# A bidirectional scan layer on one core: one conv tap of two residues moved from TensorE to VectorE, order of residues 1, 2, 3, 0, gates made one pair ahead

## The chip, the cores and the metric

One core of a Trainium2 chip runs the kernel alone. The metric is the device time of one launch in microseconds (us). It was run three times; the table below gives the median. The profile comes from one further execution, whose own span is given beside it.

## The reference, cut to what matters

The input x is (4, 128, 96, 96) in float32. Each image is normalized in 32 groups of channels, and then read as four sequences of length L = 9216: along rows (H), along columns (V), and both of these backwards. On each sequence runs the same layer:

```python
t = grouped1x1(x, in_proj_w, in_proj_b, 4)        # 128 -> 512 channels
u, gate = t[:, :256], t[:, 256:]
u = silu(u)
u = depthwise_conv(u, dw_w, kernel=5, padding=2)   # 256 channels
s = ssm_in_w @ u                                   # 32 channels
a = DMIN + (DMAX - DMIN) * sigmoid(ssm_delta_w @ u + ssm_delta_b)
bb, cc = tanh(ssm_b_w @ u + ssm_b_b), tanh(ssm_c_w @ u + ssm_c_b)
h[l] = a[l] * h[l-1] + bb[l] * s[l]                # the recurrence, as a scan
u = u + ssm_out_w @ (cc * h + ssm_d * s)
y = out_proj_w @ grouped1x1(u * sigmoid(gate), mix_w, mix_b, 4)
```

The four results, put back in image order, are joined to 512 channels, mixed to 128 by fuse_w, and added to x. All of it is float32.

## The kernel before, in words

**Tiling.** A sequence is cut into 6 steps of 16 lines (1536 positions), and within a step into 4 residues p = 0..3: the positions 4n + p, N = 384 of them. A unit is one direction, one step, one residue. A pair t holds the two units s = 0 and 1 that run at the same time: a forward sequence from its start and the matching backward sequence from the other end. Image by image, first V and then H make 8 phases of 24 pairs, 192 pairs in all. So pair t has step t // 4 and, as its residue, k = t % 4.

**Mirrored steps.** The backward sequence meets the positions of the forward one in the second half of a phase. So in_proj and silu are computed only in a phase's steps 0 to 2 ("fresh"); steps 3 to 5 read the same silus backwards, from SBUF for step 3 and through DRAM copies (kept_sil) for steps 4 and 5. In the same way the gates are computed for the first 12 pairs of a phase, ten of these twelve tiles are kept in DRAM, and the last 12 pairs take them in mirrored order.

**One pair, pair() at L797.** The parts of a pair are spread over time: front (in_proj and silu, L403 to L484) runs four pairs ahead; conv, taps and proj belong to pair t itself; ssm_out, the gating and the output product belong to pair t - 6 (LAG) and t - 7.

- The 256 conv channels come as two halves j. Half j = 1 is convolved on ScalarE and VectorE: the first tap (L648, ScalarE, into PSUM banks 0 and 1) and four taps (L650, VectorE, the last one into u). Half j = 0 is convolved on TensorE: since the sequence lies as residues, channels of 32 by 4 residues make 128 rows, and one product with a banded 128x32 matrix (conv, L610) takes all taps that lie in the same shift k of n; the taps that lie in the neighbouring shift are a second product over 64 rows (conv_less, L619). For residues 1 and 2 that second product holds two taps' rows; for residues 0 and 3 only one of the five taps lies there. ScalarE then copies the result to u (L629 or L631).
- proj (L662) multiplies u for s, delta, b and c: 16 products into banks 4 and 5, then two tanh and a copy on ScalarE (L687, L688, L693), decay and the product b * s on GpSimd (L695, L696), and scale_s on ScalarE (L705).
- recurrence (L786): in the first two pairs of a step VectorE scans the two halves of the step before (L722); GpSimd forms cc * h + d * s of pair t - 5 (outputs, L726).
- under (L509) copies u of pair t - 6 to the PSUM banks of ssm_out (0 and 1 for s = 0, 2 and 3 for s = 1); out_of (L501) adds ssm_out's product; gate (L487) makes the gates' products, ScalarE their tanh (L521), each for the pair that uses them at once; gating (L582, L597) is one VectorE instruction per unit, (gate + 1) * PSUM, written over u.
- accumulate (L742) makes the fused product of mix, out_proj and fuse for the unit gated a pair before, ScalarE copies it out of PSUM (ys, L755 or L757), and GpSimd adds it to acc, the image in SBUF (L774). Complete regions of acc leave for DRAM (L737) and are loaded with the next image (L827).

**What sets the order.** All engines' orders are written out by hand (manual_schedule); each engine executes its instructions in program order and waits on semaphores. All transfers but one are issued by SyncE, on one queue: x_in for fronts (L269) and gates (L284), the kept silus (L450, L457) and gates (L530, L538), chunks of the next image for its statistics (L383), and acc. The banks are shared: taps and ssm_out of s = 0 use 0 and 1; proj uses 4 and 5; conv uses 4 and 5 or 7 and 6, the accumulates the other two; the gates 4 to 7.

**Kinds of pair** by t % 24: 0 to 5 and 20 to 23 have a front, 8 to 17 have gates, 6 and 7 both, 18 and 19 neither.

## Time and profile before

| what | value |
|---|---|
| median of 3 runs | 1809.4 us (1809.08 to 1810.35) |
| profiled execution: span from first to last instruction | 1812.7 us |
| TensorE (PE) busy, share of the span | 99% |
| ScalarE (ACT) | 86% |
| VectorE (DVE) | 80% |
| GpSimd (POOL) | 79% |
| transfers on the SyncE queue | 317.48 MB, 54.4% of the 16 DMA engines' span |

How to read the views that follow. A group row gives line, engine, operation, the tiles written and read with their shapes, the count, then busy time in us, the mean of one in ns, and the idle time of that engine just before them with what ended it. A matmul's record is its own duration; up to four, eight or sixteen run side by side in column and row tiles, so a group's busy time is less than count times mean. A timeline row gives start and length in us, engine, line and operation, and merges neighbours of one kind (x16). A float32 product appears as two instructions, so conv's 8 products of a pair are 16. Line numbers are those of the kernel before.

### The profile page before, as it was taken

The page shows a single profiled execution, that of the slowest core. Times are in us where ns is not written, and L with a number is a line of the kernel's source. Part 1 is how long each engine was busy: PE and PEld are TensorE (multiplying, and loading weights), DVE is VectorE, ACT ScalarE, POOL GpSimd, SP SyncE. Part 2 cuts the span into 40 slices and gives each one's busy share as a digit, 9 for nine tenths or more (in the row PEclk, how much of TensorE's full clock was granted, in tenths as well). Part 3 has the DMA queues.
Part 4 walks back from the last instruction along what each step waited for, and adds up shares of the span by engine and source line. Part 5 has one row for each costly group of instructions (what it writes and reads, how often), then busy time and mean ns, then how long its engine had stood idle before and what let it go on. Part 6 is the DMA issues. An engine that isn't in the chain of part 4 may idle for free.

```text
span 1812.7 us, 56970 instructions
## 1 busy us (share of the span) xinstructions
PE 1788.9 (99%) x24090; PEld 645.3 (36%) x24090; DVE 1446.5 (80%) x1462; ACT 1567.0 (86%) x2750; POOL 1432.0 (79%) x1477
## 2 busy tenths in 40 slices
PE   6999999999999999999999999999999999999998
PEld 3333333333333333333333333333333333333333
DVE  5888878887888887877788888787877878777886
ACT  4988888998888888898988888889888888889975
POOL 3587887778778888788877888778778788887876
PEclk9999999999999999999999999999999999999999
DMA  7655463444975466344696447443477734645434
GB/s 229 183 184 196 149 185 117 163 145 142 305 246 188 159 177 204 102 145 141 204 306 225 159 161 211 138 146 119 160 232 223 249 118 150 192 122 176 148 112 175
DMA packets 148047, 321.17 MB, mean 177 GB/s; under 512 B 14160, under 2 KB 115920, under 8 KB 147792
## 3 DMA queue, kind: packets, MB, share of 16 engines
q1 hardware_dynamic: 147648, 317.48, 54.4%
q8 instruction: 190, 3.11, 0.7%
q14 instruction: 65, 0.53, 0.1%
q10 hardware_dynamic: 144, 0.04, 0.0%
HBM read 185.21 MB, written 132.25 MB: 175 GB/s over the span
## 4 chain that ended last, share of the span: by engine, by line
PE 95%; DMA 2%; DVE 2%; ACT 1%; issue 0%; SPq 0%; DVEq 0%
PE psum L134 82%; PE psum L504 8%; PE psum L491 5%; DVE psum L650 1%; DMA x_in<-in_xs 1%; DMA xs<-in_xr 1%; DMA acc<-in_xr 0%; DVE u L597 0%; DVE u L650 0%; ACT psum L512 0%; PE psum L1035 0%; ACT u L631 0%; SPq L296 0%; ACT ys L757 0%; DVE bn L387 0%
## 5 line engine op out<-in xcount | busy, mean ns | idle before, releaser
L650 DVE SCALAR_TENSOR_TENSOR psum<-sil,small,psum 128x768 f32<-128x768 f32 x576 | 589.0, 1023 | 28.4 <-ACT psum L648 3.4
L597 DVE SCALAR_TENSOR_TENSOR u<-gate,psum 128x768 f32<-128x768 f32 x376 | 350.0, 953 | 273.4 <-ACT u L629 119.0
L134 PE MATMUL psum<-u,w_fin 128*32 128x384 f32 (+1 forms) x6192 | 551.1, 485 | 1.6 <-ACT ys L755 1.2
L134 PE MATMUL psum<-u,main 128*32 128x384 f32 x6144 | 534.7, 489 | 1.5 <-DVE u L650 1.4
L774 POOL TENSOR_TENSOR acc<-ys,acc 128x384 f32<-128x384 f32 x375 | 411.6, 1119 | 24.0 <-ACT ys L757 7.9
L728 POOL TENSOR_TENSOR t<-t,t 64x384 f32<-64x384 f32 (+1 forms) x192 | 237.7, 1238 | 156.9 <-DVE t L722 73.2
L134 PEld LDWEIGHTS psum<-u,w_fin 128*32 128x32 f32 x6192 | 189.3, 109 | 319.6 <-issue 215.3
L134 PEld LDWEIGHTS psum<-u,main 128*32 128x32 f32 x6144 | 181.9, 109 | 324.7 <-issue 197.2
L512 ACT COPY psum<-u 128x768 f32<-128x768 f32 x352 | 277.3, 801 | 17.5 <-DVE u L650 11.5
L134 PE MATMUL psum<-sil,band 128*32 128x384 f32 x3072 | 285.1, 488 | 0.0
L695 POOL TENSOR_SCALAR t<-tm 64x384 f32<-64x384 f32 x191 | 176.9, 926 | 117.3 <-ACT tm L687 97.9
L729 POOL TENSOR_TENSOR t<-t,t 64x384 f32<-64x384 f32 (+1 forms) x192 | 249.1, 1297 | 15.0
L504 PE MATMUL psum<-t,main 32*128 32x384 f32 x1536 | 238.6, 513 | 1.3 <-ACT psum L512 0.6
L648 ACT ACTIVATE psum<-sil,small 128x768 f32<-128x768 f32 x191 | 173.7, 909 | 56.2 <-DVE u L597 48.0
L521 ACT ACTIVATE gate<-psum,bnorm 128x384 f32<-128x384 f32 x384 | 192.2, 584 | 26.5 <-PE psum L491 25.5
L696 POOL TENSOR_TENSOR t<-t,tm 64x384 f32<-64x384 f32 x192 | 195.3, 1017 | 15.3
L650 DVE SCALAR_TENSOR_TENSOR u<-sil,small,psum 128x768 f32<-128x768 f32 x192 | 194.9, 1015 | 7.8
L470 ACT ACTIVATE sil<-psum,bnorm 128x385 f32<-128x385 f32 x384 | 192.6, 585 | 7.1 <-PE psum L134 4.8
L134 PE MATMUL psum<-sil,less 64*32 64x384 f32 x3072 | 168.1, 495 | 0.0
L491 PE MATMUL psum<-x_in,wn 32*128 32x384 f32 x768 | 157.3, 527 | 0.0
L134 PEld LDWEIGHTS psum<-sil,band 128*32 128x32 f32 x3072 | 90.6, 109 | 169.2 <-issue 94.4
L731 POOL COPY t<-t 64x384 f32<-64x384 f32 x187 | 136.8, 731 | 11.9
(103 smaller groups left out, 1480.3 us busy)
## 6 DMA issues: line engine op xcount, KB each, us to landing
sil<-sil SPq DMA_DIRECT2D x128, 770.0 KB, 6.7
kept<-gate SPq DMA_DIRECT2D x80, 768.0 KB, 3.7
gate<-kept SPq DMA_DIRECT2D x76, 768.0 KB, 4.9
x_in<-in_xs SPq DMA_DIRECT2D x192, 96.2 KB, 2.5
out<-acc SPq DMA_DIRECT2D x48, 384.0 KB, 8.2
acc<-in_xr SPq DMA_DIRECT2D x39, 384.0 KB, 6.8
xs<-in_xr SPq DMA_DIRECT2D x72, 192.0 KB, 5.7
x_in<-in_xs SPq DMA_DIRECT2D x46, 192.5 KB, 3.5
```

Source lines behind the costliest of these rows:

```text
L134: nc.tensor.matmul(o[r, : rhs.shape[-1]], lhsT, rhs, start=start, stop=stop, skip_group_check=True)
L470: nc.scalar.activation(sils[step][:, s, j, g, :], bank(bk)[:, : N + 1], AF.Silu, bias=bn[:, 1:2] if j else bn[:, 4 + g : 5 + g],)
L491: nc.tensor.matmul(bank(to)[:, :N], stats[un["b"]][0][r, s, :], x_in[s][r, q, off : off + N], start=True, stop=True)
L504: nc.tensor.matmul(bank(ssm(bi, s) + j)[:, :N], w_so[r, bass.ts(j, P)], z[r, :], start=bi not in seeded, stop=True, skip_group_check=True)
L512: nc.scalar.copy(psum[:, ssm(bi, s) : ssm(bi, s) + 2, :N], us[bi][:, s])
L521: nc.scalar.activation(gv[:, s, j, :], bank(to[2 * s + j])[:, :N], AF.Tanh, bias=bn[:, 2 + j : 3 + j], scale=0.5,)
L597: nc.vector.scalar_tensor_tensor(v, g, 1.0, pz, ALU.add, ALU.mult)
L650: nc.vector.scalar_tensor_tensor(us[i][:, :, 1, :] if k == K - 1 else part, src, w_tap[:, k : k + 1], part, ALU.mult, ALU.add,)
L696: nc.gpsimd.tensor_mul(ta[0:64, p, :], tb[0:64, :], tm[0:64, :])
L728: engine.tensor_mul(ta[0:64, p, r], tb[64:P, r], ta[64:P, p, r])
L729: engine.tensor_add(tb[0:64, r], ta[0:64, p, r], tb[0:64, r])
L774: adder.tensor_add(part, y, part)
```

## The change

- For t from 8 on, pair() gives way to a new pair_on().
- Residues 0 and 3 ("lone" pairs, alone(p)): conv closes its accumulation, conv_less and its copy are left out, and add_lone, one VectorE instruction, multiplies the one missing tap's silus by its weight, adds conv's PSUM banks and writes u. The silus of the neighbouring residue lie on other partitions than needed; so keep_lone stores the 32 partitions of each edge residue to DRAM (edge_sil, four DMAs per fresh step), and load_lone fetches them in a layout of 128 channels by 4 slots into one buffer, once per step.
- The order of residues is 1, 2, 3, 0 (TURN), so the lone pairs are the third and the fourth of a step. The scans stay in the first two.
- The gates of pair n + 1 are made beside ssm_out of pair n, and all 12 tiles of a half phase are kept in DRAM. Those of a phase's first three pairs are made at t % 24 = 17, 18, 19 of the phase before, in a tile that the start-up weights used (shared), and fetched later. So the pairs with a front (t % 24 = 20 to 23 and 0 to 7) make no gates, and the other 12 make them all. Two of the four tanh become one 768-wide instruction.
- In every pair from 8 on, u is copied under ssm_out on ScalarE (under), never added by VectorE.
- tm has one buffer instead of two, xs three instead of four; the statistics of the next image are spread as one chunk per pair, and finished in more and smaller pieces, two per pair.

The core of the diff:

```diff
+TURN = (1, 2, 3, 0)
...
+    def alone(p):
+        return p in (0, R - 1)
...
+    def keep_lone(step):
+        for e, r in enumerate((slice(96, P), slice(0, 32))):
+            for s in range(2):
+                nc.sync.dma_start(
+                    edge_of(step)[2 * e + s].rearrange("g c n -> c g n"), sils[step][r, s, 0, :, :]
+                )
+
+    def load_lone(step):
+        lone[step] = wk.tile([P, 4, N + 1], F32, tag="lone", bufs=1, name=f"lone_{step}")
+        nc.sync.dma_start(lone[step], edge_of(step).rearrange("a g c n -> (g c) a n"))
+
+    def add_lone(i, banks):
...
+        nc.vector.scalar_tensor_tensor(
+            us[i][:, :, 0, :],
+            columns(step, slots, k),
+            w_edge[:, 1 - k : 2 - k],
+            psum[:, banks[0] : banks[0] + 2, :N],
+            ALU.mult,
+            ALU.add,
+        )
...
+    def pair_on(t):
...
+        if mirror(n + 1) is None and (n + 1) % NP > 2:
+            gated = n + 1
+            to = tile_of(gated)
+        elif t % NP in (17, 18, 19) and t + LAG + 1 < end:
+            gated = t + LAG + 1
+            to = shared()[:, : 4 * N].rearrange("p (s j n) -> p s j n", s=2, j=2)
+        banks, w = (PROJ, FRONT[:2]) if fronted else ((6, 7), PROJ)
...
+        front(t + R, FRONT)
...
+        if k == 0 and fresh(un["step"]):
+            keep_lone(un["step"])
+        if k == (1 if fresh(un["step"]) else 0):
+            load_lone(un["step"])
+        if not fronted:
+            under(bi, 1)
...
+        taps(i, range(1, K))
+        conv(i, banks, single)
+        if single:
+            add_lone(i, banks)
+        recurrence(t)
+        stats_chunks(t)
...
+        if fronted:
+            under(bi, 1)
+            under(bi, 0)
...
+        adds = [accumulate(waiting.pop(0), w[0], *adder)]
+        if not late:
+            adds[0]()
+        if not fronted:
+            if not single:
+                conv_less(i, banks)
+            under(bi, 0)
+        adds.append(accumulate(waiting.pop(0), w[1], *adder))
...
+        if fronted:
+            if not single:
+                conv_less(i, banks)
+            scale_s(i - 2)
...
+        gate_of(1, 1, 4)
+        out_of(bi, 0, 0)
+        out_of(bi, 0, 1)
+        out_of(bi, 1, 1)
+        gate_of(1, 0, 7)
+        gate_of(0, 0, 6)
+        out_of(bi, 1, 0)
+        gate_of(0, 1, 5)
+        for s in range(2):
+            gating(bi, s)
+            if s == 0 and gated is not None:
+                tanh_one(gated, to, 1, 1, 4)
+                tanh_one(gated, to, 0, 1, 5)
+        first_tap(i + 2)
+        if gated is not None:
+            tanh_both(gated, to, 0, 6)
+            nc.sync.dma_start(kept[gated // NP % 2][gated % NP], to)
...
+        proj(i, PROJ, not fronted)
+        if not fronted:
+            scale_s(i - 2)
```

More of the change, by code (lines that the diff above doesn't have):

```diff
@@ L98, in conv_preact_kernel @@
         for st in range(NS):
-            for p in range(R):
+            for k, p in enumerate(TURN):
                 for s in range(2):
@@ L365, in conv_preact_kernel @@
     kept = [
-        [dp.tile([P, 2, 2, N], F32, tag=f"kept{e}_{m}", name=f"kept{e}_{m}") for m in range(NP // 2 - 2)]
+        [dp.tile([P, 2, 2, N], F32, tag=f"kept{e}_{m}", name=f"kept{e}_{m}") for m in range(NP // 2)]
         for e in range(2)
@@ L375, in chunks_of @@
         b, k = un["b"] + 1, t % R
-        if un["order"] == "V" and b < B and k > 1:
-            return [(b, un["st"] * R + 2 * (k - 2) + e) for e in range(2)]
+        if un["order"] == "V" and b < B:
+            m = t % NP
+            first = m - 2 + (m > 10) + (m > 18)
+            return [(b, first + e) for e in range(1 + (m in (10, 18)))] if m > 1 else []
         return []
@@ L472, in silu, with silu_both @@
             bank(bk)[:, : N + 1],
+            AF.Silu,
+            bias=bn[:, 1:2] if j else bn[:, 4 + g : 5 + g],
+        )
+    def silu_both(step, g, j, b0):
+        bn = stats[units[step * UB]["b"]][1]
+        nc.scalar.activation(
+            sils[step][:, :, j, g, :],
+            psum[:, b0 : b0 + 2, : N + 1],
             AF.Silu,
@@ L492, in gate, with gate_tile @@
                          start=True, stop=True)
+    def gate_tile(n, s, j, to, c):
+        un = units[2 * n + s]
+        q, off = gate_at(un)
+        r = slice(64 * (1 - s) + 32 * j, 64 * (1 - s) + 32 * j + 32)
+        mm(bank(to), c, stats[un["b"]][0][r, s, bass.ts(c, 32)], x_in[s][r, q, off : off + N],
+           True, True)
     turning = (6, 0, 2)
@@ L608, in blocks, with conv @@
         return [sils[step][:, s if fresh(step) else 1 - s, 0] for s in range(2)]
-    def conv(i, banks):
+    def conv(i, banks, alone=False):
         step, p = units[i]["step"], units[i]["p"]
@@ L631, in conv_less, with less_both @@
             nc.scalar.copy(us[i][:, :, 0, :], psum[:, b0 : b0 + 2, :N])
+    def less_both(i, banks):
+        step, p = units[i]["step"], units[i]["p"]
+        sil, k = blocks(step), less_of(p)
+        for g in range(4):
+            for s in range(2):
+                r = less_rows(s, p)
+                mm(bank(banks[s]), g, less[r, p, g, :], columns(step, sil[s][r, g, :], k), False, True)
     def new_u(i):
@@ L660, in conv_preact_kernel, with proj @@
     qb, qc, qa, qs = (slice(MH * i, MH * (i + 1)) for i in range(4))
-    def proj(i, banks, apart=False):
+    def proj(i, banks, apart=False, between=None):
         step, p = units[i]["step"], units[i]["p"]
@@ L1116, in conv_preact_kernel @@
         start()
-        for t in range(NU // 2):
+        for t in range(LAG + 2):
             pair(t)
+        for t in range(LAG + 2, NU // 2):
+            pair_on(t)
         tail()
```

200 lines of the change are left out of this document (165 added, 35 removed).

## The prediction, made blind

> **What bounds the kernel now.** I read the profile from the top: the busy shares, then the chain that ended last.
>
> ```profile
> PE 1788.9 (99%) x24090; PEld 645.3 (36%) x24090; DVE 1446.5 (80%) x1462; ACT 1567.0 (86%) x2750; POOL 1432.0 (79%) x1477
> PE 95%; DMA 2%; DVE 2%; ACT 1%; issue 0%; SPq 0%; DVEq 0%
> ```
>
> TensorE is busy for 99% of the span of 1812.7 us and is 95% of the chain. So the time is the length of its instruction stream, and the reader should next see how one pair of units is made up. The timeline of a pair with gates but without a front (columns: start, us, engine, line):
>
> ```profile
> 353.39 0.59 PE L491 MATMUL psum<-x_in,wn 32*128 32x384 f32 x2
> 354.97 2.79 PE L134 MATMUL psum<-u,main 128*32 128x384 f32 x32
> 357.57 1.47 PE L134 MATMUL psum<-sil,band 128*32 128x384 f32 x16
> 358.86 1.47 PE L134 MATMUL psum<-u,w_fin 128*32 128x384 f32 x16
> 359.45 0.79 ACT L512 COPY psum<-u 128x768 f32<-128x768 f32 x1
> 360.26 0.88 PE L134 MATMUL psum<-sil,less 64*32 64x384 f32 x16
> 360.40 0.58 ACT L755 ACTIVATE ys<-psum,b_fin 128x384 f32<-128x384 f32 x1 [0.17 <-PE psum L134]
> 361.07 1.50 PE L134 MATMUL psum<-u,w_fin 128*32 128x384 f32 x16
> 361.25 0.80 ACT L631 COPY u<-psum 128x768 f32<-128x768 f32 x1 [0.26 <-PE psum L134]
> 361.94 0.81 ACT L512 COPY psum<-u 128x768 f32<-128x768 f32 x1
> 362.50 0.59 PE L491 MATMUL psum<-x_in,wn 32*128 32x384 f32 x2
> ```
>
> From start to start on TensorE: gates and ssm_out together ("the wave") 1.58, proj 2.60, band 1.29, first accumulate 1.40, less 0.81, second accumulate 1.43. The pair takes 362.50 - 353.39 = 9.11 us. Write O for the start of the wave. Then the copy of conv's result (L631) starts at O + 7.86, as soon as less is done, and the copy of u under s = 0 (L512) ends at 362.75, which is 0.25 after the next wave began. The old order bears that, because its two ssm_out products of s = 0 come last but one in the wave. A pair with a front and without gates, from proj to proj:
>
> ```profile
> 417.67 2.77 PE L134 MATMUL psum<-u,main 128*32 128x384 f32 x32
> 420.36 0.95 PE L134 MATMUL psum<-x_in,wn 32*32 32x385 f32 x32
> 421.24 1.50 PE L134 MATMUL psum<-sil,band 128*32 128x384 f32 x16
> 422.55 2.76 PE L134 MATMUL psum<-u,w_fin 128*32 128x384 f32 x32
> 423.64 1.54 ACT L512 COPY psum<-u 128x768 f32<-128x768 f32 x2
> 425.25 0.88 PE L134 MATMUL psum<-sil,less 64*32 64x384 f32 x16
> 426.05 0.93 PE L504 MATMUL psum<-t,main 32*128 32x384 f32 x8
> 426.91 2.79 PE L134 MATMUL psum<-u,main 128*32 128x384 f32 x32
> 427.10 1.82 DVE L597 SCALAR_TENSOR_TENSOR u<-gate,psum 128x768 f32<-128x768 f32 x2 [1.48 <-ACT u L629]
> ```
>
> That is 9.24 us, 0.80 of it less. Its two copies of u (L512) end at 425.18, just before less starts at 425.25. Of 24 pairs in a phase, ten are of each of these kinds, two have both front and gates, and two have neither. The first taps issued in pair 30 and in pair 54 give the length of a phase:
>
> ```profile
> 299.95 0.91 ACT L648 ACTIVATE psum<-sil,small 128x768 f32<-128x768 f32 x1
> 521.38 0.91 ACT L648 ACTIVATE psum<-sil,small 128x768 f32<-128x768 f32 x1
> ```
>
> 221.4 us for 24 pairs.
>
> **The change, part by part.**
>
> *Less left out.* The 184 pairs from t = 8 on hold 92 of residue 0 or 3 ("lone"). Each loses its 16 less instructions, 0.80 us of TensorE, and the copy after them: 92 x 0.80 = 74 us if TensorE alone decided.
>
> ```profile
> L134 PE MATMUL psum<-sil,less 64*32 64x384 f32 x3072 | 168.1, 495 | 0.0
> L650 DVE SCALAR_TENSOR_TENSOR u<-sil,small,psum 128x768 f32<-128x768 f32 x192 | 194.9, 1015 | 7.8
> L722 DVE TENSOR_TENSOR_SCAN t<-t,t 64x768 f32<-64x768 f32 x40 | 100.0, 2499 | 1.3
> L387 DVE BATCH_NORM_STATS2 bn<-xs 128x6 f32<-128x384 f32 x72 | 36.5, 550 | 2.3 <-DMA xs<-in_xr 2.3
> ```
>
> *The tap on VectorE.* add_lone has the form of the last tap (one SBUF tensor, one in PSUM, 128x768, into u), so 1.02 us, 92 times. It stands behind the four taps and ahead of scan, statistics and gating. With order 1, 2, 3, 0 the lone pairs are the third and fourth of a step, and the scans fall in the first and second. A lone pair then asks VectorE for four taps 4.2, add_lone 1.0, gating 1.8 and statistics 0.55 = 7.6 us, less than any pair's length. The heaviest, the first of a step, asks 4.2 + 2.5 + 1.8 + 0.55 = 9.1 us, under 9.24. So I cost add_lone at nothing; without that cover it is up to 1.0 us per lone pair.
>
> *Gates a pair ahead; who is late then.* Now no pair has both front and gates: 12 of 24 have one, 12 the other. Gating no longer waits for its own tanh. What remains is a loop through PSUM banks 0 and 1: ssm_out, gating of s = 0, first tap, four taps, copy under s = 0, next ssm_out.
>
> ```profile
> 363.44 2.00 ACT L521 ACTIVATE gate<-psum,bnorm 128x384 f32<-128x384 f32 x4 [0.28 <-PE psum L491]
> 364.53 1.90 DVE L597 SCALAR_TENSOR_TENSOR u<-gate,psum 128x768 f32<-128x768 f32 x2 [1.14 <-ACT gate L521]
> 365.52 0.91 ACT L648 ACTIVATE psum<-sil,small 128x768 f32<-128x768 f32 x1
> 366.37 0.56 ACT L687 ACTIVATE tm<-psum,small 128x384 f32<-128x384 f32 x1
> 366.46 3.14 DVE L650 SCALAR_TENSOR_TENSOR psum<-sil,small,psum 128x768 f32<-128x768 f32 x3
> 369.64 1.01 DVE L650 SCALAR_TENSOR_TENSOR u<-sil,small,psum 128x768 f32<-128x768 f32 x1
> ```
>
> In a pair with gates (O = 362.50) gating began at O + 2.0 after its tanh. Without that wait it begins as in the pair with a front, 427.10 - 426.05 = 1.05 after O, and ends s = 0 at O + 2.0. The second single tanh waits for the wave's last gate and runs from about O + 1.7 to O + 2.3, so the first tap runs to O + 3.2 (was 3.9), and the taps, 4.2 long, end at O + 7.4 (was 8.15). Then ScalarE itself is late: the new two-bank tanh (a 768-wide ScalarE instruction, 0.91 as the first tap) runs to O + 4.1, so proj's tanh begins 0.25 later than at 366.37, and all behind it too: the copy under s = 1, at O + 6.06 before, ends at 7.1; the ys copy (0.58) at 7.7; the copy under s = 0 (0.81) at 8.5.
>
> - Lone pair with gates: TensorE would need 9.11 - 0.81 = 8.30, but ssm_out of s = 0 is now second in the wave and waits for that copy: **8.5**.
> - Other pair with gates: less ends no earlier, its copy runs from 7.86 to 8.66, the copy under s = 0 ends at 9.36 as before; but now the wave's second product waits for it: 9.36 + 0.05 = **9.4**, against 9.11.
> - Lone pair with front: the copies of u are done before the accumulates end, so all of less is won: **8.44**.
> - Other pair with front: **9.24**.
>
> A phase is 6 x (8.5 + 9.4 + 8.44 + 9.24) = 213.5. For the turns from one kind to the other I add 0.5, a choice: 214, 7.4 less than 221.4 per phase, and 184/24 = 7.67 phases make **-57 us**.
>
> [...]
>
> *Copies through DRAM.* Each new step stores its silus' two edge residues in four DMAs (0.79 MB) and loads them back (0.79 MB); the mirrored step loads them again. The last two gate tiles of a half phase are now kept too, and three gate tiles are made in the phase before and fetched: with 0.79 MB each, 3 + 6 transfers for the lone tiles and 2 + 2 + 3 for the gates, 12.6 MB more per phase.
>
> ```profile
> sil<-sil SPq DMA_DIRECT2D x128, 770.0 KB, 6.7
> q1 hardware_dynamic: 10480, 23.26, 80.4%
> gate<-kept SPq DMA_DIRECT2D x6, 768.0 KB, 8.1
> GB/s 342 116 242 0 44 237 220 301 392 416 414 320 215 316 323 255 303 397 413 344 108 139 286 209 317 411 406 321 237 371 366 204 33 7 0 76 360 379 340 238
> DMA to landing us min/median/max: 1.7/3.4/13.9
> ```
>
> The first row is the page's for all such DMAs; the next three are those of the window from 440 to 530 us, where one image's output leaves and the next one's arrives; the last is that of the x_in loads. In a new step the load of the lone tile is issued behind the store of silus or gates of the step's first pair, about 5 us after that pair's wave, and first used after the third pair's taps, about 16.5 after it: 11.5 us of cover for a landing of 6.7. In old steps it is a pair earlier still. In the window the DMA share is 80%; the 5.5 MB more there (two stores, two lone loads, three gate tiles) take it to 80.4 x 28.8 / 23.3 = 99%. There I take 1 us for each of three image changes, with bounds of 0 and 5 us (twice what a landing of 13.9 overruns the cover by). Elsewhere 0.
>
> [...]
>
> *The rest.* Four gates and four single tanh are made in pair 8: 2 us, as the four at 363.44, once. With one buffer for tm, a late GpSimd would hold the next pair's first tanh; both readers of tm stand ahead of the next pair's work in its order, so 0. The statistics of an image come in two pieces per pair, products that wait for VectorE and the other way round: between 0 and half a gating (0.9) in each of some 6 pairs of three images, 16 us; I take 0, since the old pairs carried the same pieces.
>
> Sum: 1812.7 - 57 + 3 + 2 = 1760.7. The profiled span lies 3.3 above the median of the runs, 1809.4, so **1757**.
>
> **Rivals.**
>
> 1. *TensorE decides everywhere* (the ScalarE copies come out earlier than I place them). 6 x (8.30 + 9.11 + 8.44 + 9.24) + 0.5 = 211: -10.4 per phase, -80; 1812.7 - 80 + 2 - 3.3 = 1731. For it: in the old trace ScalarE is at 86%. Against it: the copy at 361.94.
> 2. *VectorE and ScalarE wait on each other.* In a first pair VectorE's 9.1 us leave 0.1. If its lateness went on into the next first tap, 0.4 us in each of 46 first pairs and 0.5 in each of 46 lone pairs with gates: +41, 1798.
> 3. *DMA late at the image changes*: 5 us at each of three, 1757 - 3 + 15 = 1769. [...]
> 4. *Slower than before: the lone tile lands late.* add_lone blocks VectorE until it has; gating, taps and the scans stand behind it. Some 22 new steps load it with a cover of 11.5 us plus 1.2 until proj needs u. At 15.8 us to landing each loses 3.1: +68, 1825. It decides against the change from 15.3 us on. For it: one SP queue issues all, and the store must have landed first; x_in loads have taken 13.9. Against it: 6.7 at the median.
>
> That the change does not do what it says would show as rival 2: the products are gone, and the loop keeps the time.
>
> **How the numbers follow.** The forecast has 0.48, rival 1 0.17, rival 2 0.10, rival 3 0.10, rival 4 0.12, and something that ends at no change 0.03. The range goes from rival 1 to rival 2, 1730 to 1798, and leaves out 0.15. Faster by over 0.2% (3.6 us, about what a measurement can tell from no change): 0.85; within: 0.03; slower: 0.12.
>
> **What would show it.** The less group at 100 x 16 = 1600 instructions; add_lone 92 times near 1.02 us. From one first tap to the next 8.4 to 8.5 in lone pairs and 9.2 to 9.4 in the others, all clearly above 8.3 where there are gates. In pairs with gates the wave's ssm_out waits for ScalarE's copy under s = 0; if that wait is gone, rival 1 holds. A wait of add_lone for a DMA near the image changes is rival 3, in every new step rival 4. I am wrong altogether if TensorE's idle time passes 80 us.

## The result, and the profile after

| kernel | median, us | runs, us | profiled span, us |
|---|---|---|---|
| before, beside the changed one | 1809.48 | 1809.08 to 1810.35 | 1812.7 |
| changed | 1784.38 | 1781.68 to 1788.70 | 1787.0 |

The ratio is 0.9863, 95% interval 0.9849 to 0.9877: 25 us faster, where 52 were forecast. The time lies inside the forecast's range, but a little over half of the gain is missing. Sums go by spans as in the prediction: 1787.0 measured against 1760.7 in its sum, so 26.3 us are to be found.

The page of the changed kernel, its span, the busy shares, and the chain that ended last by engine and by line:

```profile
span 1787.0 us, 54377 instructions
PE 1739.9 (97%) x22618; PEld 661.0 (37%) x22618; DVE 1496.9 (84%) x1526; ACT 1492.7 (84%) x2551; POOL 1423.3 (80%) x1477
PE 81%; DMA 8%; ACT 4%; DVE 3%; POOL 2%; issue 1%; SPq 1%; DVEq 0%; ACTq 0%; POOLq 0%
PE psum L135 68%; PE psum L548 8%; PE psum L528 5%; DMA kept<-shared 2%; DVE psum L765 1%; DMA x_in<-in_xs 1%; DMA out<-acc 1%; DMA lone<-edge 1%; ACT sil L498 1%; DMA edge<-sil 1%; ACT psum L560 1%; DVE u L664 1%; DMA xs<-in_xr 1%; ACT psum L763 1%; ACT shared L564 0%
```

Before, TensorE was 95% of the chain and DMA 2%. Now DMA is 8%, and three names in the second chain row are transfers that the change added or made urgent: the store of the shared gate tile (kept<-shared), the load of the lone tile (lone<-edge) and the store of its edges (edge<-sil). TensorE still has nothing to do in 47 us only, well under the 80 at which the prediction called itself wrong altogether.

The groups by line show that the change does what it says:

```profile
L135 PE MATMUL psum<-sil,less 64*32 64x384 f32 x1600 | 88.0, 497 | 0.0
L717 DVE SCALAR_TENSOR_TENSOR u<-lone,small,psum 128x768 f32<-128x768 f32 x92 | 92.8, 1008 | 8.3 <-DMA lone<-edge 5.6 <-PE psum L548 2.2 <-PE psum L135 0.5
```

1600 less instructions are left of 3072, and add_lone runs 92 times at 1.01 us (forecast 1.02).

The pair prices follow from the timeline of ScalarE, first tap to first tap (first column, us):

```profile
1392.09 0.91 ACT L763 ACTIVATE psum<-sil,small 128x768 f32<-128x768 f32 x1 [0.77 <-DVE u L664]
...
1480.26 0.90 ACT L763 ACTIVATE psum<-sil,small 128x768 f32<-128x768 f32 x1
1489.69 0.90 ACT L763 ACTIVATE psum<-sil,small 128x768 f32<-128x768 f32 x1
1497.95 0.90 ACT L763 ACTIVATE psum<-sil,small 128x768 f32<-128x768 f32 x1
1506.21 0.90 ACT L763 ACTIVATE psum<-sil,small 128x768 f32<-128x768 f32 x1
...
1578.59 0.91 ACT L763 ACTIVATE psum<-sil,small 128x768 f32<-128x768 f32 x1 [0.86 <-DVE u L664]
1587.94 0.91 ACT L763 ACTIVATE psum<-sil,small 128x768 f32<-128x768 f32 x1 [0.51 <-DVE u L664]
1597.21 0.91 ACT L763 ACTIVATE psum<-sil,small 128x768 f32<-128x768 f32 x1 [0.52 <-DVE u L664]
1605.71 0.91 ACT L763 ACTIVATE psum<-sil,small 128x768 f32<-128x768 f32 x1 [0.86 <-DVE u L664]
```

With gates: 9.43 (other), then 8.26 and 8.26 (lone). With a front: 9.35 and 9.27 (other), 8.50 (lone). The first row (pair 150) and the last (pair 174) bound the phase of the last image, in which no image follows: 213.6 us for 24 pairs, where the forecast said 214. The phases before it, measured in the same way from pair 30 on, took 216.1, 219.8, 218.5, 218.1 and 216.1. So the price of an ordinary pair came out right or nearly so; what is missing lies in a few pairs. Set against the same pairs in a kernel that has none of these waits (none_of_three, below; the statistics against an ordinary lone pair with a front, 8.50; pair 8 against the forecast), these are longer:

| where | pairs | us over |
|---|---|---|
| tanh into the shared gate tile waits for the store of the tile before | 19, 20, 67, 68, 91, 115, 116, 139, 140, 164 | 9.2 |
| statistics of the next image are finished | 27, 75, 123 | 8.2 |
| lone tile late at an image change | 50, 98, 99, 146, 147 | 6.2 |
| first pair of the new kind | 8 | 3.0 |

That is 26.6. The forecast's sum already held 3 of it for the image changes, so some 24 of the 26.3 are placed, somewhat less where a pair behind a long one comes out shorter (the pair after each statistics pair takes 8.81 instead of 9.36). The rest is not placed.

**The store of the shared gate tile.** The waits of the changed kernel (us in all, times, longest):

```profile
ACT shared L564 <- DMA kept<-shared: 10.8, 8, 3.1
...
DVE u L717 <- DMA lone<-edge: 5.6, 2, 3.0
```

A window of the timeline around pair 67 (start, length, engine, line):

```profile
627.50 0.34 SPq L1143 DMA_DIRECT2D kept<-shared  x1
...
634.77 1.05 ACT L564 ACTIVATE shared<-psum,bnorm 128x384 f32<-128x384 f32 x2 [2.40 <-DMA kept<-shared]
...
635.41 4.12 PE L135 MATMUL psum<-u,main 128*32 128x384 f32 x32 [1.91 <-ACT shared L564]
```

The tile of pair 66 leaves at 627.50, and the next tanh into the same tile can start only at 634.77, 2.40 late. Proj then starts 1.91 late. The store had 4.9 us until the tanh wanted the tile (634.77 - 2.40 - 627.50) and took about 7.2. The prediction counted this tile's transfers as bytes, but not that there is only one such tile. What follows the gap is in the same kernel's stretches of 1.5 us (busy time of the five engines with instruction counts, then the granted clock, the DMA share and GB/s):

```profile
629.00:630.50 1.50, 1.50 (x24) 0.65 (x20) 1.47 (x2) 1.41 (x3) 1.37 (x2) 1.00 1.10 404
...
633.50:635.00 1.50, 0.00 (x0) 0.00 (x0) 1.27 (x2) 0.23 (x1) 1.42 (x3) 1.00 0.86 238
635.00:636.50 1.50, 1.09 (x16) 0.52 (x20) 0.00 (x0) 1.50 (x3) 1.00 (x1) 1.00 0.79 158
636.50:638.00 1.50, 1.50 (x16) 0.46 (x12) 1.31 (x2) 1.42 (x3) 0.00 (x0) 0.57 0.88 351
638.00:639.50 1.50, 1.50 (x19) 0.26 (x14) 1.47 (x2) 0.00 (x0) 0.89 (x1) 0.50 0.96 392
639.50:641.00 1.50, 1.50 (x41) 0.53 (x42) 1.31 (x2) 1.38 (x3) 0.87 (x1) 0.79 0.89 296
```

DMA is at 0.79 to 1.10 in all of them. And after the 1.91 us in which TensorE had nothing, its granted clock falls to one half for about 3.4 us: proj takes 4.12 instead of 2.79. The clock lost over this episode is 1.5 x (0.43 + 0.50 + 0.21) = 1.71 us, nearly as much as the gap itself; it is what makes pair 68 long.

**The statistics.** The timeline around pair 27:

```profile
272.38 0.50 POOL L848 COPY t<-t 64x384 f32<-64x384 f32 x1
272.39 0.50 DVE L200 TENSOR_TENSOR dev<-mv,mean 128x1 f32<-128x1 f32 x1
...
272.93 1.26 DVE L202 SCALAR_TENSOR_TENSOR ex<-dev,mv 128x1 f32<-128x1 f32 x1
272.96 2.38 POOL L891 TENSOR_TENSOR acc<-ys,acc 128x384 f32<-128x384 f32 x2
...
274.11 1.25 DVE L204 TENSOR_SCALAR gm<-gmask,mean 128x4 f32<-128x4 f32 x1
...
275.28 1.80 DVE L664 SCALAR_TENSOR_TENSOR u<-gate,psum 128x768 f32<-128x768 f32 x2
```

Three VectorE instructions on one to four columns take 0.50, 1.26 and 1.25 us, and each ends with the GpSimd instruction beside it (0.50 and twice 1.19). Gating (L664) stands behind them, and they stand behind a copy of the mean, for which VectorE had been idle 1.16 us. Before, the groups of the same three operations had means of 0.22, 0.99 and 0.22.

**The lone tile.** The timeline around pair 50:

```profile
472.89 0.39 SPq L708 DMA_DIRECT2D lone<-edge  x1
...
481.67 1.01 DVE L717 SCALAR_TENSOR_TENSOR u<-lone,small,psum 128x768 f32<-128x768 f32 x1 [2.57 <-DMA lone<-edge]
...
482.74 2.79 PE L135 MATMUL psum<-u,main 128*32 128x384 f32 x32 [1.36 <-DVE u L717]
```

The load is issued at 472.89 and its reader starts at 481.67: 8.8 us, where the prediction had 6.7; and it is issued some 10 us after the wave of the step's first pair, not 5, because the edges' own store before it was late. The reader wanted the tile at 479.10, so 6.2 of the 11.5 us of cover were left.

**Pair 8.** TensorE in its first pair with gates ahead:

```profile
92.22 1.38 PE L528 MATMUL psum<-x_in,wn 32*128 32x384 f32 x4 [1.00 <-ACT gate L564]
...
96.37 1.35 PE L135 MATMUL psum<-sil,less 64*32 64x384 f32 x16
```

Gates wait for their tanh, and the less group takes 1.35 instead of 0.88, again at the half clock (0.50 from 94.0 to 97.0 us). The pair takes 14.4 us; 11.4 had been forecast.

### The profile page after: what moved, and what is told of

Its sections match the earlier page's. It is cut to its first block, busy times and chain, and to the rows that moved or that the text cites. A ratio compares the mean times of both kernels' runs of the same rounds, so it can differ in the third digit from the quotient of the medians.

```text
span 1787.0 us, 54377 instructions
## 1 busy us (share of the span) xinstructions
PE 1739.9 (97%) x22618; PEld 661.0 (37%) x22618; DVE 1496.9 (84%) x1526; ACT 1492.7 (84%) x2551; POOL 1423.3 (80%) x1477
## 4 chain that ended last, share of the span: by engine, by line
PE 81%; DMA 8%; ACT 4%; DVE 3%; POOL 2%; issue 1%; SPq 1%; DVEq 0%; ACTq 0%; POOLq 0%
PE psum L135 68%; PE psum L548 8%; PE psum L528 5%; DMA kept<-shared 2%; DVE psum L765 1%; DMA x_in<-in_xs 1%; DMA out<-acc 1%; DMA lone<-edge 1%; ACT sil L498 1%; DMA edge<-sil 1%; ACT psum L560 1%; DVE u L664 1%; DMA xs<-in_xr 1%; ACT psum L763 1%; ACT shared L564 0%
## 5 line engine op out<-in xcount | busy, mean ns | idle before, releaser
L765 DVE SCALAR_TENSOR_TENSOR psum<-sil,small,psum 128x768 f32<-128x768 f32 x576 | 589.0, 1023 | 51.7 <-ACT psum L763 26.3
L135 PE MATMUL psum<-u,main 128*32 128x384 f32 x6144 | 538.2, 491 | 13.8 <-ACT shared L564 7.2
L135 PE MATMUL psum<-u,w_fin 128*32 128x384 f32 (+1 forms) x6192 | 543.1, 485 | 1.6 <-ACT ys L872 0.4
L664 DVE SCALAR_TENSOR_TENSOR u<-gate,psum 128x768 f32<-128x768 f32 x376 | 341.8, 950 | 181.2 <-PE psum L548 65.8
L845 POOL TENSOR_TENSOR t<-t,t 64x384 f32<-64x384 f32 (+1 forms) x192 | 235.3, 1225 | 137.8 <-DVE t L839 84.3
L135 PEld LDWEIGHTS psum<-u,w_fin 128*32 128x32 f32 x6192 | 194.5, 110 | 313.0 <-issue 233.9
L560 ACT COPY psum<-u 128x768 f32<-128x768 f32 x380 | 298.2, 799 | 9.2 <-DVE u L664 4.4
L846 POOL TENSOR_TENSOR t<-t,t 64x384 f32<-64x384 f32 (+1 forms) x192 | 272.3, 1418 | 15.1
L548 PE MATMUL psum<-t,main 32*128 32x384 f32 x1536 | 209.6, 524 | 4.5 <-ACT psum L560 3.3
L528 PE MATMUL psum<-x_in,wn 32*128 32x384 f32 x768 | 167.9, 495 | 3.6 <-DVE shift L259 1.4
L874 ACT COPY ys<-psum 128x384 f32<-128x384 f32 x281 | 129.5, 477 | 14.9 <-PE psum L135 11.8
L564 ACT ACTIVATE gate<-psum,bnorm 128x384 f32<-128x384 f32 x148 | 85.8, 581 | 57.1 <-PE psum L528 56.8
L802 ACT ACTIVATE tm<-psum,small 128x384 f32<-128x384 f32 x192 | 111.1, 579 | 11.6 <-PE psum L135 3.4
```

Of the source, the lines that this page charges most:

```text
L135: nc.tensor.matmul(o[r, : rhs.shape[-1]], lhsT, rhs, start=start, stop=stop, skip_group_check=True)
L528: nc.tensor.matmul(bank(to)[:, :N], stats[un["b"]][0][r, s, :], x_in[s][r, q, off : off + N], start=True, stop=True)
L548: nc.tensor.matmul(bank(ssm(bi, s) + j)[:, :N], w_so[r, bass.ts(j, P)], z[r, :], start=bi not in seeded, stop=True, skip_group_check=True)
L560: nc.scalar.copy(psum[:, ssm(bi, s) : ssm(bi, s) + 2, :N], us[bi][:, s])
L664: nc.vector.scalar_tensor_tensor(v, g, 1.0, pz, ALU.add, ALU.mult)
L765: nc.vector.scalar_tensor_tensor(us[i][:, :, 1, :] if k == K - 1 else part, src, w_tap[:, k : k + 1], part, ALU.mult, ALU.add,)
```

## The experiments

The theory (A): the pair prices are as forecast, and the missing 26 us are waits in a few pairs. Rivals to it (the recorded expectations use some of the letters for rivals of their own): the less products were never worth their 0.8 us (B); the pair form with gates ahead is itself the loss (C); the transfers are late because the bytes of their stage are the limit, so no order of issue mends them (D). The runs came in three groups, each beside its own runs of the kernel before (medians 1812.47, 1812.54 and 1810.08: less_back to stats_gpsimd, changed_again to mended, and the rest); ratios stand to those. The changed kernel itself took 1784.4 in its first runs and 1794.3 as changed_again, 10 us more, so times are compared within a group, and across groups only where the difference is well above 10 us. The clock is the mean granted TensorE clock of the profiled execution.

| label | median, us | ratio, 95% interval | profiled span, us | granted clock |
|---|---|---|---|---|
| less_back | 1856.04 | 1.0245, 1.0220 to 1.0270 | 1851.7 | 0.999 |
| gates_at_once | 1822.37 | 1.0051, 1.0034 to 1.0067 | 1822.4 | 0.989 |
| split_store | 1796.30 | 0.9909, 0.9889 to 0.9929 | 1792.1 | 0.996 |
| stats_gpsimd | 1793.17 | 0.9892, 0.9873 to 0.9912 | 1792.0 | 0.994 |
| changed_again | 1794.34 | 0.9902, 0.9886 to 0.9919 | 1792.1 | 0.996 |
| no_early_store | 1784.08 | 0.9844, 0.9830 to 0.9859 | 1780.7 | 0.998 |
| none_of_three | 1768.55 | 0.9762, 0.9748 to 0.9777 | 1770.1 | 0.998 |
| mended | 1786.45 | 0.9859, 0.9844 to 0.9873 | 1784.9 | 0.996 |
| mended_again | 1781.15 | 0.9836, 0.9823 to 0.9850 | 1780.2 | 1.000 |
| mended_2 | 1793.62 | 0.9906, 0.9891 to 0.9921 | 1788.0 | 0.999 |
| gates_at_once_2 | 1794.33 | 0.9915, 0.9902 to 0.9928 | 1791.9 | 0.999 |

**The less products back (less_back).**

```diff
-        single = alone(un["p"])
+        single = False
...
-        if k == 0 and fresh(un["step"]):
-            keep_lone(un["step"])
-        if k == (1 if fresh(un["step"]) else 0):
-            load_lone(un["step"])
```

> The changed kernel with the 64-row products back in all pairs from 8 on: single is always false, so no tap is added by VectorE, and the copies of the edge silus through DRAM are left out. Order of residues, gates a pair ahead and all else stay. Theory A (the prices of the pairs were right, what is missing lies in a few places that wait): every pair with gates then takes 9.4 us and every pair with a front 9.3, so 46 x 1.1 + 46 x 0.8 = 88 us more than the changed kernel, about 1866 us with some 6 us of late lone tiles gone. Rival B (the loop through PSUM banks 0 and 1 holds the lone pairs everywhere, and leaving the products out paid little): at most 46 us more, 1830 or below.

1856.0, nearer to theory A's 1866 than to B's 1830: without the lone taps the new pair loses 2.45% on the kernel before. From first tap to first tap its pairs take 9.42 with gates and 9.26 with a front, whether the residue is lone or not, and a phase 225.3 or 226.3: twelve of each, as the prediction priced its "other" pairs. The chain shows that the waits have gone with the time to spare:

```profile
PE 91%; ACT 4%; DVE 2%; DMA 1%; issue 1%; POOL 1%; SPq 0%; DVEq 0%; POOLq 0%; ACTq 0%
```

Against changed_again (1794.3, of another group) the lone taps are worth 62 us; against none_of_three below, which has no such waits and its statistics mended too, 87.5, or at most 0.95 per lone pair. The prediction had 0.9 with gates and 0.8 with a front.

**Gates in their own pair (gates_at_once, gates_at_once_2).** The old pair with the lone tap; in the first one the lone load stands behind the reload of the accumulators, in the second ahead of it. Both have the statistics in their old pieces, and make no gate tiles for the next phase.

```diff
-            conv(i, banks)
-        if t and not ahead:
+            conv(i, banks, single)
+        if single:
+            add_lone(i, sorted(banks))
+        if t and not ahead and not single:
             conv_less(i, banks)
...
-        for t in range(LAG + 2):
+        for t in range(NU // 2):
             pair(t)
-        for t in range(LAG + 2, NU // 2):
-            pair_on(t)
```

> The old pair for all 192 pairs (gates made for the pair that uses them, statistics in the old pieces), with the new order of residues, the products of residues 0 and 3 left out and their tap added by VectorE, and all 12 gate tiles kept. Theory A: by the old rows a phase is 6 x 9.24 + 4 x 8.44 with a front, 6 x 9.11 + 4 x 8.30 with gates, 2 x 9.25 with both and 2 x 8.05 with neither, 212 us, so about 1738 to 1745 us: moving the gates ahead has cost more than it brought. Rival C (gates ahead are needed, since gating waits for its own tanh): the lone pairs with gates stay near 8.9 and the time is 1765 or above.

This run's theory A (1738 to 1745) fell, and its rival C, that gates ahead are needed, fits: 1822.4, slower than before. Lone pairs with gates take 8.80, others with gates 9.35 and 9.10, and the two pairs of a phase with both, where nothing is late, 9.8 to 10.1 and 10.8. But three pairs (50, 98, 146) are 6.5 to 7 us longer and pair 102 4.9, and the timeline around pair 50 shows why:

```profile
469.33 2.20 SPq L931 DMA_DIRECT2D acc<-in_xr  x3
...
472.32 0.38 SPq L695 DMA_DIRECT2D lone<-edge  x1
...
481.99 1.01 DVE L704 SCALAR_TENSOR_TENSOR u<-lone,small,psum 128x768 f32<-128x768 f32 x1 [7.45 <-DMA lone<-edge]
```

The reader of the lone tile waits 7.45 us for a load issued behind three reloads. So the form of the pair and the late load were mixed; hence the second trial.

> Gates in their own pair again (the old pair with the lone tap), the lone tile's load now ahead of the pair's other loads, so that the late lone tiles of the first trial of this do not hide what the form of the pair costs. By the pair prices of that trial (8.80 us with gates and a lone tap, 9.35 and 9.10 with gates alone) and without its four late pairs (some 25 us together) 1797 us. Theory A: between 1792 and 1804, so gates a pair ahead are worth some 0 to 10 us over the form before, less than half of what the lone taps are worth. Theory B: gates ahead carry the change, and this stays above 1812, the time of the kernel before. If the lone tile is late again the pairs 50, 98 and 146 show it.

1794.3, inside what theory A gave (1792 to 1804). The pair prices are unchanged (8.80, 9.35, 9.10), and pairs 50 and 98 are 1.9 and 1.4 over. Late loads, with the clock that they cost, had made some 28 us of the first trial (of another group). The page's chain of the second:

```profile
PE 69%; DVE 16%; ACT 6%; DMA 5%; issue 3%; POOL 1%; SPq 1%; DVEq 0%; ACTq 0%; POOLq 0%
```

Here VectorE is 16% of the chain, against 3% in the changed kernel: gating waits for its own tanh again, and a lone pair with gates takes 8.80 instead of 8.26. Beside mended_again of the same group (1781.2) gates ahead are worth 13 us, and that kernel also has its statistics mended. The changed kernel, with its waits, keeps little of that: its ratios are 0.9863 and 0.9902 against 0.9915 here. Rival C, that gates ahead are the loss, falls.

**The store in two halves (split_store).**

```diff
                 tanh_one(gated, to, 0, 1, 5)
+                if gated != n + 1:
+                    nc.sync.dma_start(kept[gated // NP % 2][gated % NP][:, :, 1, :], to[:, :, 1, :])
...
-            nc.sync.dma_start(kept[gated // NP % 2][gated % NP], to)
+            if gated != n + 1:
+                nc.sync.dma_start(kept[gated // NP % 2][gated % NP][:, :, 0, :], to[:, :, 0, :])
+            else:
+                nc.sync.dma_start(kept[gated // NP % 2][gated % NP], to)
```

> The changed kernel, but the gate tile that is made in the shared buffer is stored to DRAM in two halves, the half of the two single tanh as soon as these are done. Theory A: the single tanh of the next pair no longer waits for the store of the tile before, and 8 to 12 us of the three pairs before each phase's end go: about 1774 us. Rival D (the transfers are late as a whole, 30% more bytes): no change beyond 2 us.

No gain: 1796.3, where the changed kernel took 1784.4 and 1794.3 in other groups. The shared tile of split_store, ScalarE's idle time for the store (us, times), and its transfers (the stores and one load at the start) from issue to landing:

```profile
  DMA kept<-shared: 8.8, 7
...
DMA to landing us min/median/max: 3.5/5.8/11.9
```

Half the bytes do not land sooner (5.8 at the median, 5.2 for the whole tile before). But the edit did not do what theory A needed, as the timeline around pair 20 shows:

```profile
191.16 0.64 SPq L1141 DMA_DIRECT2D kept<-shared  x1
...
192.50 0.53 SPq L1146 DMA_DIRECT2D kept<-shared  x1
...
200.06 1.05 ACT L564 ACTIVATE shared<-psum,bnorm 128x384 f32<-128x384 f32 x2 [2.42 <-DMA kept<-shared]
```

L1141 stores the half that the next single tanh writes, L1146 the other. Yet the tanh at 200.06 waits for the semaphores of both stores, and the chain that ended last puts its release on the one issued at 192.50. By the trace's records the first half had landed at 199.01 and the second at 199.96, so a wait for its own half alone would have been shorter by 1 us of 2.4. The run shows late landings, as rival D has it, but doesn't decide between A and D. A second buffer for this tile was not tried.

**The statistics' small operations on GpSimd (stats_gpsimd).**

```diff
-        nc.vector.tensor_sub(dev, mv[:, 0:1], mean)
...
+            nc.gpsimd.tensor_sub(dev, mv[:, 0:1], mean)
+            nc.gpsimd.tensor_mul(ex, dev, dev)
+            nc.gpsimd.tensor_add(ex, ex, mv[:, 1:2])
+            nc.gpsimd.tensor_mul(gm4, gmask, mean.broadcast_to([P, 4]))
```

> The changed kernel, but the three small statistics instructions between the mean and the variance (128x1 and 128x4) run on GpSimd, as four instructions, in the three images that come later. Theory A: these 3 us of VectorE stand ahead of gating in a lone pair and on the loop; without them pairs 27, 75 and 123 fall from 11.2 us by about 2 each: 6 us less, 1778. Rival E (the pair waits for the statistics' product behind the ys copies, whatever VectorE does after it): 0 to 2 us less.

The first of the four in the groups by line of this kernel:

```profile
L207 POOL TENSOR_TENSOR dev<-mv,mean 128x1 f32<-128x1 f32 x3 | 0.6, 204 | 0.0
```

Four operations of 0.2 us each, and pairs 27, 75 and 123 fall from 2.7 us over to 0.5. The cause of this term is shown. The pair behind each grows from 8.81 to 9.39, so over the pairs that follow 1.5 us per image remain, some 4.6 in all. In the time it can't be seen: 1793.2 stands beside 1794.3 of another group, and pairs 91, 92 and 114, at the shared tile, were 1.8, 2.0 and 1.2 us over in that run.

**The changed kernel again, without the early store, without all three (changed_again, no_early_store, none_of_three).** changed_again is the changed kernel itself. no_early_store neither stores nor fetches the three early gate tiles; none_of_three also makes no copies of lone silus after the first and has the statistics on GpSimd.

```diff
-            nc.sync.dma_start(kept[gated // NP % 2][gated % NP], to)
+            if gated == n + 1:
+                nc.sync.dma_start(kept[gated // NP % 2][gated % NP], to)
...
     def load_lone(step):
+        if step > 2:
+            lone[step] = lone[2]
+            return
```

> The changed kernel unchanged, as the reference for the other three on this chip. All theories: 1784 us, give or take the few us by which chips differ; the wait of the single tanh for the store of the shared tile, of the lone tap for its tile near the image changes, and 11.2 us in pairs 27, 75 and 123 are seen again.

> The changed kernel, but the three gate tiles made ahead for each next phase are neither stored to DRAM nor loaded for those first three pairs, which then take what the gate buffer holds; their mirrored pairs load the first phase's tiles. So this leaves out part of the gates' data flow, all of their arithmetic stays. Theory A (few places that wait): no tanh waits for a store, pairs 18 to 20 of a phase lose their extra time, 9 to 13 us less than the changed kernel. Rival D (33 MB less in all, time follows the bytes): 33 of 414 MB, spread over every stage, with the waits for lone tiles near the image changes shorter as well; the pairs 18 to 20 keep most of their excess.

> The changed kernel without the stores and loads of the early gate tiles as in no_early_store, with the lone tile copied through DRAM for the first new step only (later steps use that tile's data), and with the small statistics on GpSimd. So it leaves out data flow, but no arithmetic except that of three small statistics is moved. Theory A: the pair prices alone remain, 8.3 and 9.4 with gates, 8.5 and 9.3 with a front: my sum without its 3 us for late transfers, 1757 - 3 = 1754, plus 3 for pair 8, which took 5 and not 2, plus some 6 for what is left of the statistics: 1760, 24 us below the changed kernel. Rival F (the loss sits in the pairs themselves): less than 12 us below.

1794.3, 1784.1 and 1768.6. The early store is worth 10.3 us, all three 25.8. Without the early store pairs 18 and 19 are back at 8.26 or 8.36, and pair 20 keeps only what the turn from gates to a front costs (10.16, against 9.27 for an ordinary pair). The waits of add_lone for its tile stay (10.5 us, 12.2 in changed_again), though 33 MB are gone, so these waits do not follow the bytes of the whole. The page of none_of_three:

```profile
PE 89%; ACT 3%; DVE 3%; POOL 1%; DMA 1%; issue 1%; SPq 0%; DVEq 0%; POOLq 0%; ACTq 0%
```

DMA is back at 1% of the chain. From pair 30 on a phase takes 214.6 to 214.8 there, 216.7 once and 213.3 without a following image; the prediction had 214. But changed_again was slower than the kernel measured first: by its span of 1792.1 it missed the sum of 1760.7 by 31.4, and none_of_three's 1770.1 still lies 9.4 above it. Pair 8 is 1.4 of that (12.78 against 11.4) and one long pair, 116, another 1.7; the rest is not placed.

**Mended, with all data flow kept (mended, mended_again, mended_2).** The statistics as above; the edges are stored at the end of the last pair of the step before, and the lone tile is fetched ahead of the next pair's front.

```diff
+        if k == 1 and fresh(un["step"]):
+            load_lone(un["step"])
         front(t + R, FRONT)
...
-        if k == 0 and fresh(un["step"]):
-            keep_lone(un["step"])
-        if k == (1 if fresh(un["step"]) else 0):
-            load_lone(un["step"])
+        if t == LAG + 2:
+            keep_lone(un["step"])
+        if k == 0 and not fresh(un["step"]):
+            load_lone(un["step"])
...
+        if k == R - 1 and fresh(un["step"] + 1):
+            keep_lone(un["step"] + 1)
```

> The changed kernel with two repairs and all data flow kept: the small statistics on GpSimd, and the edge silus stored at the end of the pair before their step and loaded ahead of the next pair's front, one pair earlier. Theory A: 6 us from the statistics and 4 to 6 from the lone tiles, 10 to 12 us below the changed kernel, the best of the kernels so far. Rival D (the transfers are late as a whole): only the 6 us of the statistics, and the lone taps wait as before.

1786.5, 7.9 below changed_again; pairs 50, 98, 99 and 146 are within 0.35 of a clean phase. Pairs 52 and 100 are now 2.5 and 2.3 over, where TensorE waits 1.5 and 1.6 us for loads of x_in: the gain of the lone tile was in part given back there. What is left is the shared tile.

> The mended kernel once more (statistics' three small operations on GpSimd, lone tiles stored and loaded a pair earlier), as the yardstick of the other two of this call. 1786 us within 5; left over: the wait of pairs 18 to 20 for the store of the shared gate tile, 8 to 11 us in all.

1781.2, and the fastest kernel here with all of its work: 0.9836 of the kernel before. Its shared tile, in the same view as that of split_store:

```profile
  DMA kept<-shared: 13.8, 9
...
DMA to landing us min/median/max: 3.7/5.4/12.3
```

In its chain DMA still has 7%, and ScalarE idles 13.8 us in all for the store. mended_2 puts that store on a queue of its own:

```diff
-            nc.sync.dma_start(kept[gated // NP % 2][gated % NP], to)
+            if gated != n + 1:
+                nc.scalar.dma_start(kept[gated // NP % 2][gated % NP], to)
```

> The mended kernel with the store of the shared gate tile issued by ScalarE, right behind the tanh that ends it, on ScalarE's own queue instead of SP's (the very first ones, of the three first tiles of a step, only where they go through the single tile; the rest stays on SP). Theory A: the store is late because it stands behind the loads of the pair before in SP's queue; on a queue of its own it lands some 4 us after its issue, the waits of ScalarE for it (10.7 us, 8 times) go, and the time falls by 7 to 10 us, to about 1778. Theory B: the bytes of that stage are the limit, whatever the queue: the waits stay within 3 us and the time within 3 us of the mended kernel. Rival C: the issue holds ScalarE, which has no time to spare in the pairs with gates: 18 pairs get longer by what an issue takes, and the time rises by 3 us or more.

1793.6, 12.5 slower, as only this run's rival C had it (3 us or more). The shared tile of mended_2, in the same view:

```profile
  DMA kept<-shared: 9.4, 8
...
DMA to landing us min/median/max: 4.3/6.4/12.8
```

The store lands later, not sooner (6.4 against 5.4 at the median), and still makes ScalarE wait. So the loads ahead of it on SP's queue were not what made it late. That its stage is short of transfer fits this, but is argued, not shown. The timeline of ScalarE in pair 42 shows what the issue itself does:

```profile
402.80 0.33 ACTq L1152 DMA_DIRECT2D kept<-shared  x1
403.23 0.58 ACT L808 ACTIVATE tm<-psum,small 128x384 f32<-128x384 f32 x1 [0.46 <-PE psum L135]
```

Proj's tanh stands behind the issue, 0.46 us after ScalarE's last work; in mended_again it follows without idle time. Pairs 42, 90 and 162, in which such an issue falls and no tanh waits for a store, take 0.28 more than in mended_again (8.64 against 8.36, and 8.54 against 8.26). Rival C of that run is thus borne out where the issue falls; the other pairs with gates, stored from SP, keep 8.26 and 9.42. The spans differ by 7.8 us, of which pairs 66 and 114 make 2.2 and 2.1 and pair 8 1.6, at half clock again; and in its chain the loads of gates (gate<-kept) have 2%. Why the loads of gates came later stays open.

## Why the prediction was right in its mechanism and wrong in its size

The steps that failed are two terms put at nothing and one put too small, all of them waits outside the ordinary pair; they are marked below.

- **TensorE as the bound, and less left out:** right. 0.67 us per lone pair with the waits that came with it, up to 0.95 without; 0.8 to 0.9 forecast. Without the lone taps there is no gain at all. (The 0.67 compares two groups.)
- **The four pair prices:** right but for one. 8.50 (8.44 forecast), 9.27 to 9.35 (9.24) and 9.42 (9.4). The lone pair with gates took 8.26, not 8.5, below the 8.3 that the prediction named as its own sign: here rival 1 was right. The timeline around that turn shows the copy under s = 0 and the two waves:

```profile
1486.60 0.81 ACT L560 COPY psum<-u 128x768 f32<-128x768 f32 x1
1487.15 0.58 PE L528 MATMUL psum<-x_in,wn 32*128 32x384 f32 x1
...
1487.55 0.60 PE L548 MATMUL psum<-t,main 32*128 32x384 f32 x3
...
1495.64 0.58 PE L528 MATMUL psum<-x_in,wn 32*128 32x384 f32 x1
...
1495.81 0.60 PE L548 MATMUL psum<-t,main 32*128 32x384 f32 x3
```

In the other pair the copy ends at 1487.41, and the first ssm_out of s = 0 starts 0.40 after the wave; in the lone pair it starts 0.17 after, next to no wait. So the wait that was forecast is there in one kind and not in the other. The copy itself was placed well: in the lone pair behind an other pair it ends 8.52 after that pair's wave began (8.5 forecast), and from wave to wave this pair takes 8.49. But the next wave then begins just as the copy ends, and the second lone pair takes 8.26, its copy ending at 8.29. The four pairs of a step take 35.4, where the forecast had 35.8. This makes good part of what the turns cost beyond 0.5 (0.9 in pair 20 alone), so that the 214 per phase is in part luck.

- **add_lone at nothing:** right. 92 x 1.01 us, and first pairs of a step, the heaviest for VectorE, keep 9.42 and 9.26.
- **"Elsewhere 0" for the copies through DRAM:** this step failed, and it is the largest. It weighed the early gate tiles as bytes at the image changes, and did not ask what a single tile does to the instruction that fills it next. Three tiles in consecutive pairs go through one buffer, so each tanh needs the store before it landed within a pair; the stage around pair 67 runs at a DMA share of 0.8 to 1.1 and the store takes up to 7.2 us. 9.2 us by pairs, the half clock behind a gap included, and 10.3 between changed_again and no_early_store, which shows it.
- **"I take 0" for the statistics, "since the old pairs carried the same pieces":** failed, 8.2 us in three pairs (some 6.5 with the shorter pairs behind them), inside the bounds of 0 to 16 that stood beside it. The same pieces stand now directly ahead of gating and beside GpSimd's adds, and wait for these. Shown by stats_gpsimd.
- **1 us per image change for the lone tile:** failed as too small, 6.2 us in all in this profile, 12.4 in changed_again, against 3 (bounds 0 to 15). The bytes did not reach what was feared: from 440 to 530 us the DMA share rose from 81% to 90%, not to 99%. Not the landing alone was off but the issue: 10 us after the wave instead of 5. Rival 4 stayed away: no wait in ordinary new steps.
- **2 us for pair 8:** 5.0, of which 1.7 is half clock.
- **Rival 2** did not come: lone pairs with gates were shorter than forecast, not 0.5 longer.

Its own test, "a wait of add_lone for a DMA near the image changes is rival 3", came true, together with two waits that it had no test for. Rival 3's time (1769) was missed all the same, since it priced the image changes alone.

## What to carry to other kernels

A change that shortens a pair takes the cover from every transfer timed by that pair: price each buffer with one copy as its refill against what the shorter pair leaves it (here 3.6 to 7.2 us to landing against 4.9 us), not as bytes in a total. Small operations ahead of the gating instruction are priced by what runs beside them on GpSimd, not by their own size (here 1.26 us on one column, beside 1.19 on GpSimd, and 0.22 with nothing beside it). And a gap of TensorE was worth up to twice its length here (1.78 us, and 1.71 of clock behind it), so waits in a few pairs are worth mending first.

## What the runs showed of the hardware that was not expected

- **After some short gaps TensorE's granted clock fell to one half.** Gaps of 1.91 and 1.78 us and the lightly filled pair 8 (idle 1.00 and 0.20 us before its gates and its accumulate) were each followed by about 3.4 us at 0.50, costing 1.71 us each and 5.1 in the profile of the changed kernel; gaps of 2.63 (at 198 us) and 1.36 (at 481) were not, nor was one of 2.80 in mended_again. In gates_at_once 18.8 us were lost so, most of what the 0.989 in its row stands for. In mended (0.996) it was 6.8, half of it in the start-up (54 to 62 us), and in mended_again (1.000) none: of the same kernel, they differ by 4.7 in span. So a gap of 1.78 us was followed by it and one of 2.80 was not: the length alone does not decide, and what does, no run here shows.
- **VectorE's smallest operations can last as long as GpSimd's instruction beside them:** the two of 128x1 took 0.50 and 1.26 us around pair 27, beside 0.50 and 1.19 on GpSimd, and 0.16 and 0.22 in the changed kernel's first image (at 20.6 and 20.8 us), where GpSimd was idle. What couples the two engines, no run here shows.
- **Smaller stores or a queue of their own did not land sooner** in a stage near full DMA share (0.92 on average over the 5.2 us behind each of the changed kernel's 21 stores, 0.64 to 1.04): 5.8 us at the median for halves, 6.4 for the store from ScalarE, 5.2 to 5.4 for the whole from SP, over all 21 tiles. Each figure is of one profile.
